# A graph layer on one core: five and four picked windows in turn for four, and 978 gathers for 1225

## The chip, the core and the metric

The kernel runs on one core of a Trainium2 chip. The metric is the device time of one execution in microseconds. The core has five engines: TensorE (PE; its weight loads are listed as PEld), VectorE (DVE), ScalarE (ACT), GpSimd (POOL) and SyncE (SP). Each works through its own list of instructions in order and waits for the others by semaphores.

## The reference

400,000 edges, sorted by `dst`, join 12,500 nodes with 128 features each. Every edge sends its source row through one of two linear maps, by its type; the messages are summed per destination; a self term is added, then relu, residual and a layer norm.

```python
Xs = X[src]
m_data = Xs @ W_data.T + b_data
m_ctrl = Xs @ W_control.T + b_control
msg = jnp.where((edge_types == 0)[:, None], m_data, m_ctrl)
agg = jax.ops.segment_sum(msg, dst, num_segments=X.shape[0])
out = agg + (X @ W_self.T + b_self)
x = _layernorm(x + jax.nn.relu(out), axis=-1)
```

## The kernel before, in words

The sum over edges is taken before the linear maps: for each node and type the kernel sums source rows, and multiplies by the weights once per node. `x` is split into three bf16 parts that add up to the float32 value and is held twice: in SBUF as `x3` (98 blocks of 128 nodes) and in DRAM as `rows3`.

**Tiles, groups, windows.** 128 edges make a tile; 3125 tiles make 25 groups `g` of 125 tiles, which cover 500 nodes each. A group is cut into windows, one after the other in `dst`: "p" windows of 12, 11, 11, 11 tiles (`PC`) and "e" windows of 20 tiles (`EC`), in turn. The two kinds get their source rows in two ways.

*Gathered* ("p", `gathered`): for each tile GpSimd issues an indirect DMA (L700) that fetches 128 rows from `rows3` into a `msg` tile, and PE adds them into a PSUM window `sums` by three matmuls with a one-hot matrix `psel` (L658) and one for the counts (L712). 1125 tiles go this way. The `msg` pool has `AHEAD` = 24 buffers; a gather is listed where its tile is used, and POOL may run ahead in its list as far as buffers are free.

*Picked* ("e", `picked`): PE itself takes rows out of `x3`. The 2560 edges of a window are sorted into 100 cells of 32 places, one cell per block of nodes (`give_slots`: a chain of DVE work with small PE products: `before` L537, `ranks` L547 on, `rank_matrix`, `over`, then `put` L601 and `spread` L609, which writes a table to DRAM and broadcasts it back as `pick`, 800 KB). Matmuls with the one-hot `pick` as weights give the rows in PSUM (`got` L732, 98 matmuls, four side by side), ACT casts them to bf16 (`emsg` L743, 12 casts of two row groups), and PE adds them into another `sums` window (L658, 72 matmuls and 3 for spares; counts L761). Up to 64 edges that find no place ("spares") are fetched by one gather on POOL (`last`, L747).

**Order.** One e window and the p tiles listed beside it are a *pair*; there are 100, and the work order is written out in Python: each stream yields units with a place between 0 and 1, and `merged` sorts them by place. `picked` has seven units (steps): unit t lists the `got` matmuls and casts of four row groups, the counts and the `sums` of the unit before; the seventh unit has no `got`, only the last `sums`, the `tiled` work of a later window at key 6 (`turn_codes` L621, the spares' `turn` L489 and `keep_codes` L631, L496, L498) and `accumulate`. Meanwhile the slots of the window two pairs ahead are computed. Tiles of p windows start at pair `LAG` = 2.

`got` has two PSUM buffers of two banks, `sums` two of one bank, `emsg` five buffers, `esel` and `psel` (one-hot matrices from DVE, L463) two each. `accumulate` (L688) adds a finished `sums` window into `acc[g]` on DVE at an offset read from `place_i`; `finish` multiplies by the weights, normalizes and writes 500 rows (L837, L850 and on).

**First part.** ACT's queue loads `x` and the weights, SP the indices: first `dst` of every window (`first_i`, from which DVE computes `halves` L340, `node0` and `place_i`), `near_i`, the edges of group 0. `x` is split while the slots of windows 0 and 1 are made; then `rows3` is stored.

Of the kernel before, what the change touches and what calls it, by code (L numbers as in the profile page):

```python
# [17 lines left out]
P = 128  # L18
D = 128
# [6 lines left out]
PC = (12, 11, 11, 11)  # L26
PB = 12
EC = 20
CQ = EC // 4
NE = len(PC)  # L30
# [6 lines left out]
AW = PW + DPC * (PB - 1)  # L37
# [9 lines left out]
AHEAD = 24  # L47
ACC_ROWS = 99 * P
EPS = 1e-5

assert sum(PC) + NE * EC == GC and NC % GC == 0 and NBLK == NCELL - 2 and max(PC) == PB

# [16 lines left out]
):  # L69

# [78 lines left out]
def short_path(ctx, tc, const, ident, eps, wT, brow, bad, x, src, dst, etype, ws, bs, out):  # L149
# [12 lines left out]
    def windows(g):  # L162

        c = g * GC
        for i, n in enumerate(PC):
            yield "p", i, c, n
            yield "e", i, c + n, EC
            c += n + EC
# [4 lines left out]
    rows_p = NE * PB  # L173
    raw = {}
    starts = {k: [c for kind, _, c, _ in windows(0) if kind == k] for k in "pe"}
    assert all(b - a == 31 for k in "pe" for a, b in zip(starts[k][k == "p":], starts[k][1 + (k == "p"):]))

    def load(g, kind):
        names = ("src", "dst", "typ")
        if kind == "e":  # L180
            raw[kind, g] = [ld.tile([P, NE, EC], I32, name=f"e{name}") for name in names]
            c = g * GC + starts["e"][0]
            for t, a in zip(raw[kind, g], (src, dst, etype)):
                at = a[c * P:(c + 31 * (NE - 1)) * P].rearrange("(i k) -> i k", k=31 * P)[:, :EC * P]
                nc.sync.dma_start(out=t[:, :NE - 1, :], in_=at.rearrange("i (p c) -> p i c", c=EC))
                nc.sync.dma_start(out=t[:, NE - 1, :], in_=edges(a, c + 31 * (NE - 1), EC))
        else:
            raw[kind, g] = [ld.tile([rows_p, P], I32, name=f"p{name}") for name in names]
            c = g * GC
            for t, a in zip(raw[kind, g], (src, dst, etype)):  # L190
                nc.sync.dma_start(out=t[:PB, :], in_=a[c * P:(c + PB) * P].rearrange("(c p) -> c p", p=P))
                for i in range(1, NE):
                    b = c + starts["p"][i]
                    nc.sync.dma_start(
                        out=t[i * PB:(i + 1) * PB, :], in_=a[b * P:(b + PB) * P].rearrange("(c p) -> c p", p=P)
                    )


    first_i = keep.tile([1, NG, NWIN], I32, name="first_i")

    def load_first(kind):
        for i, (k, _, c, _) in enumerate(windows(0)):
            if k == kind:
                nc.sync.dma_start(
                    out=first_i[:, :, i:i + 1],
# [9 lines left out]
    for kind, i, c, _ in windows(0):  # L215
        if kind == "p":
            nc.sync.dma_start(
                out=near_i[i * PB:(i + 1) * PB, :],
                in_=dst.rearrange("(o g e) -> o g e", o=1, g=NG)[:, :, c * P].to_broadcast([PB, NG]),
            )  # L220
# [52 lines left out]
    for i, (w, b) in enumerate(zip(ws, bs)):  # L273
        nc.scalar.dma_start(out=wn[:, i, :], in_=w)
        nc.scalar.dma_start(out=brow[:, i, :], in_=b.rearrange("(o d) -> o d", o=1))
# [59 lines left out]
    over_n = keep.tile([P, NG * NE], BF, name="over_n")  # L335

    halves = tmp.tile([1, 2, NG * NWIN], I32, name="halves")
    nc.vector.memset(x3[:, NBLK - 1], 0.0)
    first = first_i.rearrange("o g w -> o (g w)")
    nc.vector.tensor_single_scalar(halves[:, 0, :], first, 7, op=OP.logical_shift_right)  # L340
    nc.vector.tensor_single_scalar(halves[:, 1, :], first, 127, op=OP.bitwise_and)
    halves_b = tmp.tile([1, 2, NG * NWIN], BF, name="halves_b")
    nc.vector.tensor_copy(halves_b, halves)
    fin0 = ps1.tile([P, 512], FP, name="fin")
    for i in range(2):
        nc.tensor.matmul(fin0[:, :NG * NWIN], scale[:, i, :], halves_b[:, i, :], start=(i == 0), stop=(i == 1))
    node0 = keep.tile([P, NG, NWIN], FP, name="node0")
    nc.vector.tensor_copy(node0, fin0[:, :NG * NWIN].rearrange("p (g w) -> p g w", w=NWIN))
    near = keep.tile([rows_p, NG], FP, name="near")
    from_i = tmp.tile([rows_p, 1], I32, name="from_i")  # L350
    from_f = tmp.tile([rows_p, 1], FP, name="from_f")
    nc.gpsimd.iota(from_i, pattern=[[0, 1]], base=-PAD, channel_multiplier=DPC)
    nc.vector.tensor_copy(from_f, from_i)
    for k in range(1, NE):
        ge = raw[f"ge{k}"] = tmp.tile([rows_p, 1], FP, name=f"ge{k}")
        nc.vector.tensor_scalar(
            ge, from_f, float(DPC * PB * k - PAD), float(-DPC * PB), op0=OP.is_ge, op1=OP.mult
        )
    for k in range(1, NE):
        nc.vector.tensor_add(from_f, from_f, raw.pop(f"ge{k}"))  # L360
    nc.vector.tensor_scalar(near, near_i, from_f, None, op0=OP.add)
    place = tmp.tile([1, 2, NG, NWIN], FP, name="place")
    ref = tmp.tile([1, NG, NE, 2], I32, name="ref")
    nc.gpsimd.iota(ref, pattern=[[GN, NG], [0, NE], [-PAD, 2]], base=PAD - M0, channel_multiplier=0)
    ref = ref.rearrange("o g e k -> o g (e k)")
    least = tmp.tile([1, NG, NWIN], FP, name="least")
    for i, (_, _, c, _) in enumerate(windows(0)):
        nc.vector.memset(least[:, :, i:i + 1], float(max(0, c * DPC - PAD)))
    nc.vector.tensor_tensor(place[:, 0], first_i, ref, op=OP.subtract)
    nc.vector.tensor_tensor(place[:, 1], place[:, 0], least, op=OP.max)  # L370
    nc.vector.tensor_scalar(place[:, 1], place[:, 1], float(R - WMAX), None, op0=OP.min)
    place_i = keep.tile([1, NG, NWIN], I32, name="place_i")
    nc.vector.tensor_copy(place_i, place[:, 1])
    nc.vector.tensor_tensor(place[:, 0], place[:, 0], place[:, 1], op=OP.not_equal)
    nc.vector.tensor_reduce(worst[0:1, 2, 0:1], place[:, 0].rearrange("o g w -> o (g w)"), AX.X, OP.max)

    wps = ps1.tile([P, 512], FP, name="fin")
    for i in range(3):
        nc.tensor.transpose(wps[:, i * D:(i + 1) * D], wn[:, i, :], ident)
    nc.scalar.copy(wT, wps[:, :3 * D].rearrange("p (i d) -> p i d", d=D))  # L380
# [36 lines left out]
    def prep_p(g):  # L417
# [6 lines left out]
        def first():  # L424
            nc.vector.tensor_copy(sf, s)
            nc.vector.tensor_scalar(rel, d, near[:, g:g + 1], None, op0=OP.subtract)
# [12 lines left out]
    def prep_e(g):  # L439
# [3 lines left out]
        for i in range(NE):  # L443
            cs = slice(i * EC, (i + 1) * EC)
            nc.vector.tensor_scalar(rel[:, cs], d[:, cs], node0[:, g, 2 * i + 1:2 * i + 2], None, op0=OP.subtract)
# [59 lines left out]
    def give_slots(w):  # L505
        g, i = divmod(w, NE)
# [127 lines left out]
        s["tiled"] = {5: [put, spread], 6: [turn_codes, keep_codes]}  # L634
# [13 lines left out]
    acc, added = {}, []  # L648
# [27 lines left out]
    def pass_on(g):  # L676

        if g + 1 < NG:
# [3 lines left out]
    def accumulate(g, i, ps, wide, width):  # L682

        begin_acc(g)
        with tc.issue_after(added[-2].ins) if len(added) > 1 else ExitStack():
            at = nc.vector.value_load(place_i[0:1, g, i:i + 1], min_val=0, max_val=R - WMAX)
        win = acc[g][:, :, bass.ds(at, width)]
        added.append(nc.vector.tensor_add(win, win, ps[:, :4 * wide].rearrange("p (a w) -> p a w", w=wide)[:, :, :width]))  # L688

    def gathered(g, i):  # L690
        n = PC[i]
        s = {}

        def choose():
            sel = sp.tile([P, n, 2 * PW], BF, name="psel")
            s["sel"] = select(sel, near_col, codes["p", g][1][:, i * PB:i * PB + n])

        def chunk(c):
            msg = mp.tile([P, 3 * D], BF, name="msg")
            nc.gpsimd.indirect_dma_start(  # L700
                out=msg, out_offset=None, in_=rows3[:, :],
                in_offset=bass.IndirectOffsetOnAxis(ap=codes["p", g][0][:, i * PB + c:i * PB + c + 1], axis=0),
            )
# [7 lines left out]
            add_rows(rows, msg, sel, c == 0, c == n - 1)  # L711
# [6 lines left out]
    def picked(w, tiled):  # L718

        g, i = divmod(w, NE)  # L720
# [44 lines left out]

        def unit(t):

            if t < turns:
                for q in range(t * per, (t + 1) * per, pair):
                    rows(q)  # L770
            if t == 0:
                choose(0)
            if t == 1:
                choose(8)
# [3 lines left out]
            if 0 < t < turns:  # L778
                for q in range((t - 1) * per, t * per if t < turns - 1 else NQ):
                    count(q)  # L780
            if t < turns:
                for u in tiled.get(t, []):
                    u()
            if t == turns - 1:
                last_rows()
            if t > 0:
                for q in range((t - 1) * per, t * per if t < turns else NQ):
                    add_rows(cells_of(s["ps"], EW, 0), s["msg"].pop(q), s["sel"][q], False, q == NQ - 1)
            if t == turns:
                for u in tiled.get(t, []):  # L790
                    u()
                accumulate(g, 2 * i + 1, s["ps"], EW, EW)

        turns = (NQ - 1) // per
        return evenly([lambda t=t: unit(t) for t in range(turns + 1)])
# [3 lines left out]
    soon = {NE - 2: (0, 1), NE - 1: (2, 3, 4)}  # L799
    assert (starts["p"][NE - 1]) * DPC - PAD >= 2 * (P - 3)  # L800
# [86 lines left out]
    pairs = NG * NE  # L887
# [14 lines left out]

    prep_e(0)
    merged(evenly(all_slots(0) + all_slots(1)), evenly(split_units))
# [5 lines left out]
    mp = ctx.enter_context(tc.tile_pool(name="msg", bufs=AHEAD))  # L910
# [6 lines left out]
    for u in prep_p(0):  # L917
        u()


    chunks, closed, rest = {}, {}, []
    for p in range(pairs):
        g, i = divmod(p, NE)
        for c, (_, u) in enumerate(gathered(g, i)):
            at = LAG + (p + (c + 0.5) / PC[i]) * (pairs - LAG) / pairs
            chunks.setdefault(int(at), []).append((at % 1, u))
        closed.setdefault(int(at), []).append(p)

    for w in range(pairs):
        g, i = divmod(w, NE)  # L930
# [3 lines left out]
        if i == 2 and g + 1 < NG:  # L934
# [9 lines left out]
        if w + 3 < pairs:  # L944
            more += [(0.55, lambda: [u() for u in begin_slots(w + 3)])]
# [178 lines left out]
```

## Time and profile before

| | |
|---|---|
| runs before | 2387.49 us median of 3 (2369.49 to 2400.51) |
| the profiled execution | 2371.03 us, its span 2369.3 us, mean granted clock 0.909 |
| PE, DVE, ACT, POOL busy | 1863.1, 1584.0, 1229.7, 1412.5 us |
| first `got` of pair 0, 1, 2 | 76.7, 93.2, 142.6 us |
| first `got` of pair 98, 99 | 2323.9, 2338.2 us |
| gathers on POOL | 1125 of tiles (mean 1147 ns) and 100 of spares (mean 1181 ns) |

The profile is of one execution. Busy times are sums over the span; matmuls overlap and their ends are modelled, so PE's busy time is no measure of its full rate. Lines read: source line, engine, operation, output <- input, count, then busy us, mean ns, idle us before, and what ended most of that idle time. In the timeline an entry is start, length, engine, line, operation, count, and in brackets the idle time before it with what ended it. "issue" is time in which an engine waited for nothing that the profile shows.

### The profile page before, as it was taken

The page shows a single profiled execution, that of the slowest core. Times are in us where ns is not written, and L with a number is a line of the kernel's source. Part 1 is how long each engine was busy: PE and PEld are TensorE (multiplying, and loading weights), DVE is VectorE, ACT ScalarE, POOL GpSimd, SP SyncE. Part 2 cuts the span into 40 slices and gives each one's busy share as a digit, 9 for nine tenths or more (in the row PEclk, how much of TensorE's full clock was granted, in tenths as well). Part 3 has the DMA queues.
Part 4 walks back from the last instruction along what each step waited for, and adds up shares of the span by engine and source line. Part 5 has one row for each costly group of instructions (what it writes and reads, how often), then busy time and mean ns, then how long its engine had stood idle before and what let it go on. Part 6 is the DMA issues. An engine that isn't in the chain of part 4 may idle for free.

```text
span 2369.3 us, 70786 instructions
## 1 busy us (share of the span) xinstructions
PE 1863.1 (79%) x28867; PEld 1364.9 (58%) x28867; DVE 1584.0 (67%) x4224; ACT 1229.7 (52%) x2322; POOL 1412.5 (60%) x1243
## 2 busy tenths in 40 slices
PE   0468887887878787888888887888888888887977
PEld 0346665665556565666565565665666665665646
DVE  6747676766666666767676766676667666676753
ACT  3435554555445545545555554555555555545635
POOL 0366665756465565665666665566666665676661
PEclk9879898999889899999999988998989999999979
DMA  7423342333333333333323323333323323233321
GB/s 206 148 80 104 97 107 84 109 91 98 87 96 96 100 100 90 109 97 94 108 85 106 107 86 102 97 98 106 107 83 104 102 88 102 89 101 105 97 87 42
DMA packets 185017, 236.73 MB, mean 100 GB/s; under 512 B 80295, under 2 KB 152282, under 8 KB 184682
## 3 DMA queue, kind: packets, MB, share of 16 engines
q0 software_dynamic: 57200, 115.59, 17.7%
q1 hardware_dynamic: 114418, 109.94, 14.8%
q10 hardware_dynamic: 13064, 6.60, 1.0%
q8 instruction: 228, 3.74, 0.7%
q14 instruction: 107, 0.88, 0.1%
HBM read 215.35 MB, written 16.64 MB: 98 GB/s over the span
## 4 chain that ended last, share of the span: by engine, by line
PE 66%; issue 10%; ACT 10%; DVE 6%; another core or an unknown queue 5%; DMA 1%; SPq 1%; DVEq 0%; ACTq 0%; POOL 0%; POOLq 0%
PE sums L658 32%; PE got L732 22%; ACT emsg L743 9%; PE fin L850 3%; PE rk L601 2%; PE sums L761 2%; PE rk L489 1%; PE sums L712 1%; DVE esel L463 1%; PE rk L537 1%; DVE x L249 1%; PE rk L621 1%; DVE xt L247 0%; PE fin L837 0%
## 5 line engine op out<-in xcount | busy, mean ns | idle before, releaser
L700 POOL DMA_INDIRECT msg<-rows,pidx x1125 | 1290.4, 1147 | 790.3 <-PE sums L658 363.4
L743 ACT CAST emsg<-got 128x768 bf16<-128x768 f32 x1200 | 919.8, 804 | 796.5 <-PE got L732 328.8
L732 PE MATMUL got<-x,pick 128*32 128x384 bf16 x9800 | 659.2, 353 | 238.7 <-ACT emsg L743 145.6
L658 PE MATMUL sums<-esel,emsg 128*128 128x176 bf16 x7200 | 751.3, 255 | 48.6 <-issue 46.0
L658 PEld LDWEIGHTS <-emsg 128*128 128x128 bf16 x7200 | 579.8, 104 | 220.0 <-issue 215.4
L463 DVE TENSOR_TENSOR esel<-code_col,code 128x1408 bf16<-128x1408 bf16 (+1 forms) x300 | 275.0, 917 | 348.9 <-PE sums L658 195.7
L732 PEld LDWEIGHTS <-pick 128*32 128x32 bf16 x9800 | 242.3, 97 | 421.3 <-issue 336.0
L658 PE MATMUL sums<-psel,msg 128*128 128x48 bf16 x3375 | 240.0, 187 | 48.0 <-issue 35.3
L658 PEld LDWEIGHTS <-msg 128*128 128x128 bf16 x3375 | 187.8, 99 | 77.6 <-issue 72.5
L747 POOL DMA_INDIRECT last<-rows,idx x100 | 118.1, 1181 | 139.4 <-DMA pdst<-in_dst_dram 91.4
L712 PE MATMUL sums<-psel,one_col 128*128 128x48 bf16 x1125 | 184.5, 185 | 16.9 <-issue 16.8
L688 DVE TENSOR_TENSOR acc<-acc,sums 128x352 f32 (+1 forms) x200 | 94.0, 470 | 132.5 <-PE sums L658 54.0
L761 PE MATMUL sums<-esel,one_col 128*32 128x176 bf16 x2500 | 168.2, 254 | 16.2 <-issue 14.7
L463 DVE TENSOR_TENSOR O<-cell_col,blk 128x2000 bf16<-128x2000 bf16 x100 | 119.3, 1193 | 55.7 <-PE got L732 27.8
L643 DVE TENSOR_SCALAR pick<-pick,lane_f 128x1600 bf16<-128x1600 bf16 x200 | 125.6, 642 | 14.2 <-DMA pick<-there 13.7
L601 PE MATMUL rk<-rv,O 128*128 128x64 bf16 x2000 | 89.0, 198 | 50.3 <-DVE rv L589 35.0
L761 PEld LDWEIGHTS <-one_col 128*32 128x32 bf16 x2500 | 84.2, 103 | 63.7 <-issue 31.1
L547 DVE TENSOR_REDUCE ahead<-rk 128x100 bf16<-128x500 f32 x100 | 67.5, 675 | 78.7 <-PE got L732 55.7
L712 PEld LDWEIGHTS <-one_col 128*128 128x128 bf16 x1125 | 109.6, 97 | 18.0 <-issue 17.7
L551 DVE TENSOR_TENSOR prod<-O,ahead 128x2000 bf16<-128x2000 bf16 x100 | 119.0, 1190 | 0.0
L601 PEld LDWEIGHTS <-O 128*128 128x128 bf16 x2000 | 73.4, 101 | 67.3 <-issue 54.8
L631 ACT CAST code<-rk 128x50 bf16<-128x50 f32 x100 | 20.3, 203 | 173.8 <-PE got L732 68.0
(170 smaller groups left out, 1998.4 us busy)
## 6 DMA issues: line engine op xcount, KB each, us to landing
pick<-there SPq DMA_DIRECT2D x100, 800.0 KB
msg<-rows,pidx POOLq DMA_INDIRECT x1125
rows<-x SPq DMA_DIRECT2D x6, 1344.0 KB
xs<-in_x_dram SPq DMA_DIRECT2D x99, 62.5 KB
out_dram<-h SPq DMA_DIRECT2D x99, 62.5 KB
xt<-in_x_dram ACTq DMA_DIRECT2D x6, 896.0 KB
psrc<-in_src_dram SPq DMA_DIRECT2D x100, 6.0 KB
pdst<-in_dst_dram SPq DMA_DIRECT2D x100, 6.0 KB
```

The costliest lines, as they stand in the source:

```text
L463: nc.vector.tensor_tensor(sel.rearrange("p n (w t) -> p n w t", t=2), col[:rows].rearrange("p (o w t) -> p o w t", o=1, t=2).to_broadcast( ...
L551: nc.vector.tensor_tensor(prod, s["O"], ahead.rearrange("p (o j) -> p o j", o=1).to_broadcast([P, EC, NCELL]), op=OP.mult)
L601: nc.tensor.matmul(s["rk"][:m, :2 * CAP], s["held"][:, c * NCELL:c * NCELL + m], s["rv"][:, c].rearrange("p v r -> p (v r)"), start=(c == ...
L643: nc.vector.tensor_scalar(t, t, lane_f, None, op0=OP.is_equal)
L658: nc.tensor.matmul(out, msg[:, j * D:(j + 1) * D], sel, start=(start and j == 0), stop=stop, skip_group_check=True)
L688: added.append(nc.vector.tensor_add(win, win, ps[:, :4 * wide].rearrange("p (a w) -> p a w", w=wide)[:, :, :width]))
L700: nc.gpsimd.indirect_dma_start(out=msg, out_offset=None, in_=rows3[:, :], in_offset=bass.IndirectOffsetOnAxis(ap=codes["p", g][0][:, i * P ...
L712: nc.tensor.matmul(cnt, one_col, sel, start=False, stop=(c == n - 1), skip_group_check=True)
L732: nc.tensor.matmul(ps[CAP * a:CAP * (a + 1), :], slots[w]["pick"][:, a * NQ + q, :], x3[:, 4 * q + a - a0].rearrange("p j d -> p (j d)"), ...
L743: nc.scalar.copy(msg, ps[:, :, :3 * D])
L747: nc.gpsimd.indirect_dma_start(out=msg[:OVF, :], out_offset=None, in_=rows3[:, :], in_offset=bass.IndirectOffsetOnAxis(ap=slots[w]["idx"], ...
L761: nc.tensor.matmul(cells_of(s["ps"], EW, 1)[CAP * (q % 4):CAP * (q % 4 + 1), :], one_col[:, :CAP], s["sel"][q], start=(q < 4), stop=(q + 4 ...
```

## The change

Every p window now has 5 tiles (`PB`), and a group five e windows of 20; but in odd groups the fifth e window is joined to the p window before it, which then has 25 tiles (`PL`). So 13 groups have five picked windows and 12 have four: 113 pairs. 865 tiles are gathered, and with 113 spare gathers POOL issues 978. Gathers are listed 14 tiles before their use (`AHEAD`) into 18 buffers (`HOLD`). `picked` has six units, and its last sums, the `tiled` work of key 6 and `accumulate` go into `ending`, which the first unit of the next pair calls after its `got` matmuls; `put` moves from unit 5 to unit 4, `spare_rows` from unit 1 to unit 2, and `prep_p` of the next group from pair 2 to pair 1 of a group. In the first part the weights move from ACT's queue to SP's, the first `dst` of e and p windows get tiles of their own, `near`, `place_i` and the weights' transposes are made at the end of the split, and the first piece of `x` is split ahead of all else.

```diff
-PC = (12, 11, 11, 11)
-PB = 12
+PB = 5
+PL = 25
-NE = len(PC)
+NE = 5
-AHEAD = 24
+SB = 1
+HOLD = 18
+AHEAD = 14
...
+    def of_p(g, i):
+        return PL if g % 2 and i == NE - 1 else PB
+    each_e = [(g, i) for g in range(NG) for i in range(NE - g % 2)]
...
-    first_i = keep.tile([1, NG, NWIN], I32, name="first_i")
+    first_i = {k: keep.tile([1, NG, NE], I32, name=f"first_{k}") for k in "ep"}
...
-        nc.scalar.dma_start(out=wn[:, i, :], in_=w)
-        nc.scalar.dma_start(out=brow[:, i, :], in_=b.rearrange("(o d) -> o d", o=1))
+        nc.sync.dma_start(out=wn[:, i, :], in_=w)
+        nc.sync.dma_start(out=brow[:, i, :], in_=b.rearrange("(o d) -> o d", o=1))
...
-        s["tiled"] = {5: [put, spread], 6: [turn_codes, keep_codes]}
+        s["tiled"] = {4: [put, spread], 6: [turn_codes, keep_codes]}
...
+    to_fetch = [(g, i, c) for g in range(NG) for i in range(NE) for c in range(0, of_p(g, i), SB)]
+    fetched = []
+    def fetch():
+        if to_fetch:
+            g, i, c = to_fetch.pop(0)
+            msg = mp.tile([P, SB, 3 * D], BF, name="msg")
+            for k in range(min(SB, of_p(g, i) - c)):
+                at = i * PB + c + k
+                nc.gpsimd.indirect_dma_start(...)
+            fetched.append(msg)
...
         def chunk(c):
-            msg = mp.tile([P, 3 * D], BF, name="msg")
-            nc.gpsimd.indirect_dma_start(...)
+            if c % SB == 0:
+                fetch()
+                s["msg"] = fetched.pop(0)
...
         def unit(t):
-            if t < turns:
-                for q in range(t * per, (t + 1) * per, pair):
-                    rows(q)
...
+            for q in range(t * per, (t + 1) * per, pair):
+                rows(q)
+            if t in (0, 1):
+                choose(8 * t)
+            if t == 0:
+                ending()
+            if t == 2:
                 spare_rows()
...
+        def end():
+            add((turns - 1) * per, NQ)
+            for u in tiled.get(turns, []):
+                u()
+            accumulate(g, 2 * i + 1, s["ps"], EW, EW)
...
+    split_units.pop(0)()
     prep_e(0)
-    merged(evenly(all_slots(0) + all_slots(1)), evenly(split_units))
+    merged([(0.97, places_and_weights)], evenly(all_slots(0) + all_slots(1)), evenly(split_units))
...
+    for _ in range(AHEAD):
+        fetch()
...
+        units, ending = picked(w, tiled, ending)
```

## Prediction

> **What bounds the kernel now.** I read the page first: the busy shares, then the chain that ended last.
>
> ```profile
> span 2369.3 us, 70786 instructions
> PE 1863.1 (79%) x28867; PEld 1364.9 (58%) x28867; DVE 1584.0 (67%) x4224; ACT 1229.7 (52%) x2322; POOL 1412.5 (60%) x1243
> PE 66%; issue 10%; ACT 10%; DVE 6%; another core or an unknown queue 5%; DMA 1%; SPq 1%; DVEq 0%; ACTq 0%; POOL 0%; POOLq 0%
> L700 POOL DMA_INDIRECT msg<-rows,pidx x1125 | 1290.4, 1147 | 790.3 <-PE sums L658 363.4
> ```
>
> PE carries two thirds of the chain, POOL nothing: its gathers mostly wait for PE to free a buffer (363.4 us). Taken so, the change is wrong: it moves 260 tiles from the engine at 60% to the one at 79%. But 15% of the chain is time that no shown work explains ("issue", "unknown queue"), so I went on to the pace of single pairs. A pair starts at its first `got` matmul in the timeline. From pair 2 (142.6) to pair 98 (2323.9) that is 2181.3/96 = 22.72 us each. Some are far off, and the stages show what differs:
>
> ```profile
> core 0: us, PE busy (x) PEld busy (x) DVE busy (x) ACT busy (x) POOL busy (x), PEclk, DMA share, GB/s
> 142.60:157.80 15.20, 15.01 (x284) 11.61 (x280) 13.88 (x35) 10.46 (x20) 13.64 (x5) 1.00 0.20 65
> 157.80:188.00 30.20, 22.32 (x290) 14.00 (x290) 16.10 (x49) 11.46 (x22) 21.18 (x20) 0.77 0.33 93
> 2229.30:2246.20 16.90, 15.47 (x288) 11.73 (x284) 14.01 (x34) 11.79 (x27) 7.80 (x6) 1.00 0.34 98
> 2246.20:2278.70 32.50, 24.07 (x283) 14.99 (x280) 13.96 (x33) 10.30 (x21) 21.05 (x19) 0.68 0.34 97
> 2301.60:2323.90 22.30, 19.09 (x316) 15.24 (x314) 14.71 (x46) 12.40 (x27) 13.24 (x12) 1.00 0.30 92
> 2323.90:2338.20 14.30, 13.89 (x258) 10.59 (x259) 5.40 (x11) 10.23 (x19) 1.33 (x1) 1.00 0.29 88
> ```
>
> Each row is one pair (start, end and length, then the engines' busy time): the same matmuls, but 15 to 17 us where POOL got 5 or 6 gathers through and 30 to 33 us where it got 19 or 20; the granted clock falls from 1.00 to 0.7. Is POOL the cause, or does a long pair merely leave room for more gathers? The pair at 2229.3 tells, since there POOL was held by something outside PE, the indices of the next group (`pcol`):
>
> ```profile
> 2238.99 0.95 POOL L700 DMA_INDIRECT msg<-rows,pidx  x1 [6.66 <-ACT pcol L414]
> ...
> 2262.81 0.94 POOL L700 DMA_INDIRECT msg<-rows,pidx  x1 [0.30 <-issue]
> 2264.06 0.94 POOL L700 DMA_INDIRECT msg<-rows,pidx  x1 [0.30 <-issue]
> ```
>
> PE ran through undisturbed while POOL stood still. Then POOL caught up, a gather every 1.25 us, and PE fell to one or two matmuls at a time with nothing shown to wait for:
>
> ```profile
> 2262.24 0.75 PE L658 MATMUL sums<-esel,emsg 128*128 128x176 bf16 x4 [0.54 <-issue]
> 2263.65 0.45 PE L658 MATMUL sums<-esel,emsg 128*128 128x176 bf16 x2 [0.67 <-issue]
> 2265.07 0.20 PE L658 MATMUL sums<-psel,msg 128*128 128x48 bf16 x1 [0.89 <-issue]
> ```
>
> So a gather has a price on PE that its own row does not show. The reading stands on few pairs; the rivals take that up.
>
> **The price of one gather.** Between the last two stages of that episode: (32.5 - 16.9)/(19 - 6) = 1.20 us. Between the first two pairs of the table: (30.2 - 15.2)/(20 - 5) = 1.00. Between the mean of the two quiet pairs (16.05 us, 5.5 gathers) and the mean pair (22.72 us; 1225/100 = 12.25 gathers and some 0.6 that straddle a border): 6.67/7.35 = 0.91. The pair with one gather (14.3) against its neighbour with 12 gives 8.0/11 = 0.73, but it has also lost the work on later pairs (DVE 5.4 instead of 14.7). The changed pair lies between the quiet and the mean one, so I take 0.9. The upper end is 1.2; the lower is 0, if gathers only follow the pace. Below nothing is excluded: one gather less adds no work to any engine.
>
> The Trainium skill speaks against it: "SBUF — State Buffer", section "SBUF: two separate sides", says that on the engines' side only the port pair that VectorE and GpSimd share contends, and that PE and ACT never wait on another engine there. By that rule the price is 0 and the sum 2510 us, by the rows 0.9 and 2155. The rows above disagree with the rule, or have a cause that it doesn't speak of.
>
> **The change, part by part.**
> *Pairs and gathers.* 113 pairs for 100. Each brings 98 `got`, 75 `sums`, 25 counts and 36 smaller matmuls, 11.1 us of ACT, 14.6 us of DVE (their rows for the pick path, 1107.5 and 1462.8 us, over 100), 2 DMA issues on SP with one 800 KB broadcast, and one spare gather. The mean pair holds all that, so pairs x pace counts it. Gathers per pair: 1225/100 = 12.25 before, 978/113 = 8.65 after: 3.6 x 0.9 = -3.24 us.
> *PE's own work on gathered tiles.* 11.25 per pair before, 865/113 = 7.65 after. Two neighbours in the timeline start 0.10 us apart:
>
> ```profile
> 1204.86 0.24 PE L658 MATMUL sums<-psel,msg 128*128 128x48 bf16 x3
> ...
> 1204.96 0.23 PE L658 MATMUL sums<-psel,msg 128*128 128x48 bf16 x3
> ```
>
> 3.6 x 0.10 = -0.36.
> *Finishing.* 25 batches as before over more pairs: the rows of L837 and L850 are 162 us, 1.62 a pair and then 1.44: -0.19.
> *Joined steps.* At the end of a pair PE adds the last rows while ACT has no cast to do, and ACT then stands before `code`:
>
> ```profile
> 1220.17 0.83 PE L732 MATMUL got<-x,pick 128*32 128x384 bf16 x16
> ...
> 1221.40 0.20 ACT L631 CAST code<-rk 128x50 bf16<-128x50 f32 x1 [2.97 <-PE sums L658]
> ```
>
> In the quiet pair of 142.6 the seventh step took 3.27 us and the next first step 1.46, 4.73 together. Joined, PE has 16 `got` (0.66), 27 `sums` at 0.073 (2.0) and the two short turns (0.5): 3.2, a gain of 1.5. Over all pairs the two take 3.67 + 2.37 = 6.0, so up to 2 may go. The lower end is 0, where the chain through DVE takes over. I take 0.9: ACT's casts (0.80 each, two a step) still set a floor of 1.6 in every step.
> *Gathers listed in front.* Eighteen buffers for 24, listed 14 tiles ahead: 14 x 18/7.65 = 33 us before use, far more than POOL's hold of 6.66 above. PE waited 2.1 us in all for gathers before; I price it at nothing, and a hold of POOL over 33 us would return in full. The spare gather stands one step later, `put` one step earlier; both have a step (some 3 us) of room.
> *38 more adds into acc* (238 for 200) of about 0.42 us and index work on 100 columns for 80 lie on DVE, which has 14 to 15 us of work in a pair of 18; without that room 38 x 0.42/113 = 0.14 a pair. The 3 more loads a group on SP (0.4 each) lie in SP's waits for `cell` (997.8 us).
> Pair: 22.72 - 3.24 - 0.36 - 0.19 - 0.9 = 18.03 us.
> *New first part.* DVE's first real work waited for first indices which stood behind other loads on SP:
>
> ```profile
> 18.06 0.25 DVE L340 TENSOR_SCALAR halves<-first_i 1x200 int32<-1x200 int32 x1 [4.53 <-DMA first_i<-in_dst_dram]
> ```
>
> Now only the five "e" ones, first on SP, are waited for; the other places and the weights (six issues, 2.5 us of ACT's queue, now on SP behind 15 index loads) are not needed until the end of the part. That is worth up to 8 us, or nothing where the loads of `x` set the end. Pairs 0 and 1 ended at 142.6 in a burst of 26 gathers (96 to 132 us); now 14 are listed, then two spare ones that pair 0's end waits for: (16 x 1.25) = 20 us after the stored rows, so about (96 - 8) + 20 = 108, and 20 more for pair 1. I put pair 2 at 130 (120 to 143).
> Sum: 130 + 109 pairs (2 to 110) x 18.03 = 1965, + the tail as before, 2369.3 - 2323.9 = 45.4: 2140. Around the span lie 1.7 us (2371.03): 2142. The profiled run is 0.7% under the median of the runs, 2387.49; times 1.007 this is 2157, rounded 2155.
>
> **Rivals.**
> 1. *Slower: gathers only follow PE.* Price 0: 21.27 x 109 + 177 = 2495, 2510 with the factor. For it: POOL is at 0% of the chain, and a longer pair has room for more gathers. Against it: the hold by `pcol`, which PE did not cause. It decides below a price of p where 109 x (21.27 - 3.6p) + 177 = 2371, p = 0.32. Chance 0.16.
> 2. *DVE takes PE's place.* It works 14 us a pair in order, and `esel` already idles 3.5 us a pair, mostly for PE's sums; its buffers now come free in the next pair's first step. If the join brings nothing and each pair gains 1 us there: 19.93 x 109 + 177 = 2349, 2366 with the factor: no change. Against it: DVE had 13.88 of 15.20 us in the quiet pair. Chance 0.14, a half of it under 2340.
> 3. *More than forecast.* Price 1.2 and a join of 1.5: 16.35 x 109 + 177 = 1959, 1973; with only one of the two about 2040. Chance 0.08.
>
> **How the numbers follow.** The forecast (2155; own range 2050 to 2300) has 0.62. The range of 2040 to 2400 leaves out rival 1 and the best of rival 3. Faster by over 2% (under 2340; 2% is about what runs of this kernel can tell): 0.62 + 0.08 + 0.06 = 0.76; within 2%: 0.08; slower: 0.16.
>
> **What would show it.** 113 pairs of about 18 us; POOL with 978 gathers and some 1130 us busy; pair 2 near 130; no 2.97 us hole of ACT between pairs; a mean clock over 0.909; fewer "issue" and "unknown" shares. If pairs stay at 21 us with 8 or 9 gathers each, the price was wrong; at 19 to 20 us with `esel` waiting longer, the join was.

## The result, and the profile after

The changed kernel takes 2159.6 us (median of four runs, 2150.6 to 2164.9) where the kernel before takes 2378.5 in the same comparison: a ratio of 0.908, 95% interval 0.902 to 0.913. The forecast was 2155. That ratio belongs to the chip on which it was measured: on another chip of the same type it is 0.995 (e9). The experiments are mostly about this difference.

The page of the profile after, the lines that answer to those of before:

```profile
span 2163.1 us, 75401 instructions
PE 1860.4 (86%) x30869; PEld 1392.9 (64%) x30869; DVE 1730.8 (80%) x4707; ACT 1359.2 (63%) x2556; POOL 1305.9 (60%) x996
PE 61%; DVE 19%; ACT 9%; issue 5%; DMA 2%; another core or an unknown queue 1%; POOL 1%; DVEq 0%; SPq 0%; ACTq 0%; POOLq 0%
L715 POOL DMA_INDIRECT msg<-rows,pidx x865 | 1155.4, 1336 | 752.8 <-PE sums L671 316.3
```

PE has 2002 more matmuls and is busy for 2.7 us less. What went is time without shown work: "issue" and "unknown queue" fall from 15% of the chain to 6%. VectorE comes up from 6% to 19%: it is next in line. A gather's own row got longer, 1336 ns for 1147, so POOL is busy for 1305.9 us, not for the 1130 that were said. It grows on the quicker chips told of below too, from 1192 (e12) to 1314 ns (e9). The Trainium skill ("SBUF — State Buffer", section "SBUF: two separate sides") has GpSimd's descriptor writes wait while VectorE, in a two-port mode, holds the port pair that they share. VectorE's busy share did rise, but no run here tells that this is the cause.

Three pairs of the changed kernel in the stage view (length, then busy time of PE, weight loads, DVE, ACT, POOL, the granted clock, DMA share, GB/s); they got 25, 7 and 11 gathers:

```profile
103.17:142.35 39.18, 18.19 (x260) 13.67 (x260) 16.06 (x47) 10.10 (x17) 25.96 (x25) 0.70 0.34 92
744.58:760.84 16.26, 14.82 (x267) 11.20 (x264) 12.53 (x31) 10.12 (x19) 12.64 (x7) 1.00 0.34 93
1894.07:1915.75 21.68, 17.55 (x265) 12.61 (x262) 12.81 (x31) 10.10 (x19) 13.08 (x11) 0.84 0.27 90
```

A pair with many gathers is still long at a low clock, as before, but such pairs are rare now: from pair 3 to pair 110 none has more than 11 gathers started in it, where before 83 of 95 pairs had 12 or more. The seam between two pairs, from the timeline:

```profile
1207.01 0.83 PE L762 MATMUL got<-x,pick 128*32 128x384 bf16 x16
1208.24 0.18 ACT L644 CAST code<-rk 128x50 bf16<-128x50 f32 x1
```

`code` has no idle time before it here (2.97 us in the example of before), and the next pair's rows are already out. Over all pairs the time from ACT's last cast of a pair to the first of the next falls from 4.7 to 1.5 us.

### The profile page after: what moved, and what is told of

The parts are those of the page before. It is cut to its first block, busy times and chain, and to the rows that moved or that the text cites. A ratio compares the mean times of both kernels' runs of the same rounds, so it can differ in the third digit from the quotient of the medians.

```text
span 2163.1 us, 75401 instructions
## 1 busy us (share of the span) xinstructions
PE 1860.4 (86%) x30869; PEld 1392.9 (64%) x30869; DVE 1730.8 (80%) x4707; ACT 1359.2 (63%) x2556; POOL 1305.9 (60%) x996
## 4 chain that ended last, share of the span: by engine, by line
PE 61%; DVE 19%; ACT 9%; issue 5%; DMA 2%; another core or an unknown queue 1%; POOL 1%; DVEq 0%; SPq 0%; ACTq 0%; POOLq 0%
PE sums L671 27%; PE got L762 22%; ACT emsg L773 6%; PE rk L614 3%; DVE esel L476 3%; PE fin L885 2%; PE sums L791 2%; DVE prod L564 2%; DVE rv L602 1%; DVE pick L656 1%; PE rk L502 1%; PE rk L550 1%; DMA pick<-there 1%; DVE found L573 1%
## 5 line engine op out<-in xcount | busy, mean ns | idle before, releaser
L715 POOL DMA_INDIRECT msg<-rows,pidx x865 | 1155.4, 1336 | 752.8 <-PE sums L671 316.3
L773 ACT CAST emsg<-got 128x768 bf16<-128x768 f32 x1356 | 1035.8, 802 | 513.3 <-PE got L762 310.0
L762 PE MATMUL got<-x,pick 128*32 128x384 bf16 x11074 | 713.3, 335 | 136.8 <-ACT emsg L773 110.6
L671 PE MATMUL sums<-esel,emsg 128*128 128x176 bf16 x8136 | 782.6, 244 | 6.1 <-issue 5.8
L476 DVE TENSOR_TENSOR esel<-code_col,code 128x1408 bf16<-128x1408 bf16 x339 | 308.8, 911 | 43.9 <-PE sums L671 36.2
L703 DVE TENSOR_TENSOR acc<-acc,sums 128x352 f32 (+2 forms) x238 | 102.0, 428 | 211.6 <-PE sums L671 153.3
L671 PE MATMUL sums<-psel,msg 128*128 128x48 bf16 x2595 | 188.0, 185 | 9.5 <-issue 5.0
L777 POOL DMA_INDIRECT last<-rows,idx x113 | 146.2, 1294 | 70.6 <-DVE idx L513 24.4
L671 PEld LDWEIGHTS <-msg 128*128 128x128 bf16 x2595 | 150.9, 98 | 21.0 <-issue 16.1
L476 DVE TENSOR_TENSOR O<-cell_col,blk 128x2000 bf16<-128x2000 bf16 x113 | 135.0, 1194 | 21.6 <-PE got L762 10.7
L741 PE MATMUL sums<-psel,one_col 128*128 128x48 bf16 x865 | 145.9, 184 | 3.8 <-issue 3.7
L791 PEld LDWEIGHTS <-one_col 128*32 128x32 bf16 x2825 | 99.2, 98 | 51.5 <-issue 18.2
```

The lines of the kernel that those rows point to most:

```text
L476: nc.vector.tensor_tensor(sel.rearrange("p n (w t) -> p n w t", t=2), col[:rows].rearrange("p (o w t) -> p o w t", o=1, t=2).to_broadcast( ...
L671: nc.tensor.matmul(out, msg[:, j * D:(j + 1) * D], sel, start=(start and j == 0), stop=stop, skip_group_check=True)
L715: nc.gpsimd.indirect_dma_start(out=msg[:, k, :], out_offset=None, in_=rows3[:, :], in_offset=bass.IndirectOffsetOnAxis(ap=codes["p", g][0] ...
L741: nc.tensor.matmul(cnt, one_col, sel, start=False, stop=(c == n - 1), skip_group_check=True)
L762: nc.tensor.matmul(ps[CAP * a:CAP * (a + 1), :], slots[w]["pick"][:, a * NQ + q, :], x3[:, 4 * q + a - a0].rearrange("p j d -> p (j d)"), ...
L773: nc.scalar.copy(msg, ps[:, :, :3 * D])
```

## The experiments

The runs fell on four chips, and beside each group of them the kernel before ran on the same chip. The chips are of two kinds. The kernel before takes 2434.6 us on chip 0 and 2383.0 on chip 14, as in the profile shown first: kind A. It takes 1986.7 and 1985.0 us (at two times) on chip 1 and 1967.8 on chip 5: kind B. The expectations of e1 to e8 were written before this was known, with the times of kind A in mind.

**e1 to e4, on chip 1 (before: 1986.7).** e1 is the changed kernel with four picked windows in every group:

```diff
-        return PL if g % 2 and i == NE - 1 else PB
+        return PL if i == NE - 1 else PB
-    each_e = [(g, i) for g in range(NG) for i in range(NE - g % 2)]
+    each_e = [(g, i) for g in range(NG) for i in range(NE - 1)]
```

(From the order of its code, it finishes some nodes of the last group before their last windows are added; the work is otherwise as it should be.)

> The changed kernel, but with four picked windows in every group (100 pairs and 1125 + 100 gathers, as many as in the kernel before), so that only the joined steps, the new first part and the longer list stay. Theory (a gather costs PE 0.9 us, a gathered tile 0.10): the changed kernel's pace of 18.2 us with 8.65 gathers becomes 18.2 + 3.6 x 1.0 = 21.8 us with 12.25; 98 x 21.8 + 142 + 50 = 2330 us, 2290 to 2370. Rival (gathers only follow PE, the joined steps brought everything): pace stays at 18.2 to 18.6, 98 x 18.4 + 192 = about 2000 us.

Measured: 2052.0 us, ratio 1.033 (1.026 to 1.040): slower than the kernel before on this chip, and far under the theory's 2330. PE waits 186.5 us for `last`, the spare gather; in e2, with fewer gathers, 15.4 us.

e2 has five picked windows in every group: `of_p` returns `PB` always, and `each_e` runs over all `NE`.

> The changed kernel, but with five picked windows in every group: 125 pairs and 625 + 125 = 750 gathers. Theory: 6 gathers a pair instead of 8.65 take 2.65 x 1.0 off 18.2, so 15.6 us a pair, 123 x 15.6 + 192 = 2110 us, were it not for VectorE, which has 14.6 us of work in a pair; by the changed kernel's own pairs (17.2 us with 7 gathers, 18.3 with 9) a pair with 6 takes 16.7, 2245 us. So 2110 to 2250. Rival (price 0): 123 x 18.2 + 192 = 2430 us. Rival (VectorE sets the end from here on): above 2250.

Measured: 2109.9 us, ratio 1.061 (1.057 to 1.065). The number is at the lower edge of the range said, but not for the reason said: the kernel before is quicker here too. VectorE holds 52% of e2's chain and a pair takes 16.1 us, so VectorE sets the pace, as the last rival had it, though not above 2250.

e3 takes the joined steps out of the changed kernel:

```diff
-        return evenly([lambda t=t: unit(t) for t in range(turns)]), end
+        return evenly([lambda t=t: unit(t) for t in range(turns)] + [end]), lambda: None
```

> The changed kernel with the joined steps undone: the last rows and the accumulation stand in a seventh step of their own again. Theory: the join is worth 0.9 us a pair, 113 x 0.9 = 100 us, so 2260 us (2240 to 2290). If the join only moved work from one wait to another: 2160. If it was worth the 2 us that the steps allow at most: 2385.

Measured: 1964.5 us, ratio 0.987 (0.984 to 0.991).

e4 puts the joined steps into the kernel before: `ending` of the last pair is called in a pair's first step, after `choose(0)`, and the seventh step is gone.

> The kernel before with the joined steps alone (same 100 pairs and 1225 gathers, same first part, list as before). Theory: 0.9 us x 100 pairs off 2380, so 2290 us (2200 to 2330; the kernel e1 with four picked windows everywhere should be near it). If the join is worth nothing without fewer gathers: 2380. If gathers cost nothing and the join did all: about 2000.

Measured: 2070.7 us, ratio 1.041 (1.038 to 1.045): slower. PE waits 199.6 us for `last`, the spare gather, which the joined first step needs while POOL still has others ahead of it; that is 39 us more than in the kernel before on a chip of kind B (e12), of 84 us to explain. The rest is open.

Three of the four (e1, e3, e4) lie far below what the price of 0.9 us gives, the fourth fits for another reason, and in none of the four profiles does "issue" stand among PE's larger waits. That raised the question of what the gathers do on the first chip.

**e5 to e8, on chip 0 (before: 2434.6).** e5 and e6 are the kernel before with one gather for two tiles, or for a whole window:

```diff
-            msg = mp.tile([P, 3 * D], BF, name="msg")
-            nc.gpsimd.indirect_dma_start(
+            if c % 2 == 0:    # e6: c % 12
+                s["msg"] = mp.tile([P, 3 * D], BF, name="msg")
+                nc.gpsimd.indirect_dma_start(
...
+            msg = s["msg"]
```

> The kernel before with one gather for every two gathered tiles (600 + 100 gathers instead of 1125 + 100); PE, DVE and ACT do the same work, and every second tile uses the rows of the one before it, which is what it leaves out. Theory (0.9 us a gather): 525 x 0.9 = 470 us less, about 1900 us; a floor of 15 to 16 us a pair (the quiet pairs) would give 1700 to 1800. Rival (gathers only follow PE): 2370, unchanged.

> The kernel before with one gather for a whole window of 11 or 12 tiles (100 + 100 gathers); the other tiles use its rows, which is what it leaves out. PE, DVE and ACT do the same work. Theory: 1025 x 0.9 = 920 us less by the price alone, but DVE's 14.6 us and the quiet pairs' 15 us are a floor, so 1600 to 1750 us. Rival (price 0): 2370.

Measured: 2127.2 us, ratio 0.875 (0.860 to 0.891), and 1836.8 us, ratio 0.756 (0.742 to 0.770). PE, DVE and ACT do the same work as before; only gathers are gone. So a gather costs, and does not merely follow: 307/525 = 0.58 us each in e5, 598/1025 = 0.58 in e6. Both forecasts by 0.9 (about 1900, and 1600 to 1750) were too low. But the mean hides the form of the price. Three pairs in a row of e5, in the stage view, with 1, 17 and 7 gathers:

```profile
1894.89:1913.88 18.99, 18.57 (x322) 15.33 (x320) 16.73 (x50) 13.83 (x29) 1.17 (x1) 1.00 0.15 53
1913.88:1946.28 32.40, 22.48 (x284) 14.18 (x282) 13.71 (x33) 11.80 (x26) 17.74 (x17) 0.74 0.32 88
1946.28:1961.76 15.48, 15.19 (x281) 11.38 (x278) 13.65 (x33) 10.08 (x21) 11.04 (x7) 1.00 0.28 88
```

Seven gathers in a pair cost next to nothing (the first of the three is long because it also finishes nodes, 322 matmuls); seventeen cost (32.40 - 15.48)/(17 - 7) = 1.7 us for each one more. All of e5 from pair 3 on says the same: its 39 pairs with 4 to 7 gathers take 16.4 us on the mean, its 21 pairs with 12 or more take 29.1 us (28 pairs with up to 3 take 19.0; the finishing of nodes falls mostly into these). The price is that of gathers that follow one another closely. Four lines of that pair's timeline:

```profile
1924.15 0.95 POOL L701 DMA_INDIRECT msg<-rows,pidx  x1 [0.30 <-issue]
1924.87 0.27 PE L763 MATMUL sums<-esel,one_col 128*32 128x176 bf16 x3 [1.09 <-issue]
1925.41 0.94 POOL L701 DMA_INDIRECT msg<-rows,pidx  x1 [0.30 <-issue]
1926.31 1.05 PE L658 MATMUL sums<-esel,emsg 128*128 128x176 bf16 x5 [0.99 <-issue]
```

e7 and e8 ask which part of a gather it is. They replace the 865 gathers of the changed kernel, by a plain load and by a memset:

```diff
-                nc.gpsimd.indirect_dma_start(
-                    out=msg[:, k, :], out_offset=None, in_=rows3[:, :],
-                    in_offset=bass.IndirectOffsetOnAxis(ap=codes["p", g][0][:, at:at + 1], axis=0),
-                )
+                nc.sync.dma_start(out=msg[:, k, :], in_=rows3[at * P:at * P + P, :])    # e7
+                nc.gpsimd.memset(msg[:, k, :], 0.0)                                     # e8
```

(In e7 `at` is first shifted by `(g * 45) % 90`, so that the blocks loaded differ from group to group.)

> The changed kernel with its 865 gathers of edge rows replaced by plain loads of the same 128 rows x 768 bytes, issued by SP, into the same buffers (it leaves out the choice of the rows). The transfers' bytes stay, GpSimd's work on the indices goes (113 spare gathers are left). If the price comes with the transfer into SBUF: 2160 us, unchanged. If it comes with GpSimd's making of the gather: 113 x 15 + 190 = about 1900 us (1850 to 1980).

> The changed kernel with its 865 gathers of edge rows replaced by a GpSimd memset of the same buffers (it leaves out the rows themselves): GpSimd still writes SBUF between the same waits, no transfer is made. If the price comes with the gather in either of its parts (indices or transfer): 1850 to 1980 us, as few as with plain loads or fewer. If it comes with any work of GpSimd beside PE and its waits: 2160.

Measured: 1962.6 us, ratio 0.807 (0.793 to 0.822), and 1958.5 us, ratio 0.806 (0.791 to 0.820). The changed kernel as it is was not run on chip 0; by its ratio of 0.908 it would take about 2210 there. The DMA queues of the changed kernel (first two lines; packets, MB, share of 16 engines) and of e7 (last two) show that the 85 MB only changed queue:

```profile
q1 hardware_dynamic: 125770, 121.51, 17.9%
q0 software_dynamic: 45136, 90.65, 15.1%
q1 hardware_dynamic: 250330, 206.60, 36.1%
q0 software_dynamic: 3616, 5.56, 1.3%
```

With the same bytes moved by plain loads the price is gone, and without any transfer the time is much the same; in both runs no "issue" row is left among PE's waits. So the price is neither the bytes moved nor GpSimd's plain writing into SBUF (865 memsets of 0.43 us each): it comes with GpSimd's making of an indirect transfer, or with what that transfer's queue does that a plain one does not. Those two were not separated. The form of the transfer goes with the queue: a plain load reads neighbouring rows, in 144 packets a tile where a gather has 48. The Trainium skill's page "Perfetto Trace Analysis" (section "DMA Instruction — SWDGE (GPSIMD)") says that a row of such a gather ends when the descriptors are made, not when the data has landed; by that the bursts that spoil PE's pace are seen at their source. No run here shows where such a row ends.

**e9 and e10, on chip 1 (before: 1985.0).** e9 is the changed kernel as it is, e10 is e3's kernel.

> The changed kernel again, beside the kernel before. Theory after e1 to e8: on the chip where the kernel before takes 2370 to 2435 us a gather holds PE's signals back, and the ratio is again 0.90 to 0.92; on the chip where it takes 1987 us it doesn't, VectorE sets the pace, and the changed kernel takes 1960 to 2000 us there, a ratio of 0.985 to 1.005. Rival (the price of a gather is the same everywhere, that call was quick for another reason): a ratio of 0.90 to 0.92 on either chip, 1800 us beside 1987.

> The changed kernel with the joined steps undone, beside the changed kernel itself. By the pace: of the 4.49 us that a pair lost, 3.6 gathers at the 0.585 us that e5 gave make 2.1, PE's own work and the finish 0.55; the 1.8 left would be the join, so 113 x 1.8 = 200 us over the changed kernel on the chip where a gather has a price (2360 beside 2160). By the forecast's 0.9: 2260. Rival (the join is worth nothing, the price of a gather is 1.1): 2160. On the chip without a price: 1965, the changed kernel within 2% of it.

Measured: e9 1972.6 us, ratio 0.995 (0.993 to 0.998); e10 1965.2 us, ratio 0.990 (0.988 to 0.993). Both are as forecast for a chip without a price. On a chip of kind B the change gains half a per cent, and its joined steps cost about as much; both lie within the 2% that the prediction counts as no change.

**e11, on chip 14 (before: 2383.0).** The same kernel without the joined steps.

> The changed kernel with the joined steps undone, once more, for the chip where the kernel before takes 2370 to 2435 us, to size the join there. If the join is worth the 1.8 us a pair that the other terms leave, 2360 us, a ratio of 0.99 to the kernel before; by the forecast's 0.9 us 2260, 0.95; if it is worth nothing 2160, 0.91. On the chip where that kernel takes 1985 us: 1965 again.

Measured: 2252.1 us, ratio 0.945 (0.938 to 0.952). The changed kernel was not run on this chip; at 0.908 it would take 2163, so the join is worth 89 us or 0.79 a pair: near the forecast's 0.9, not the 1.8 that I had come to after e5 by taking its mean price for every gather.

**e12, on chip 5 (before: 1967.8).** The kernel before, unchanged, for its profile on a chip of kind B.

> The kernel before, unchanged, for its profile on the chip where it takes 1985 us. Theory: there PE has next to no idle time of the kind 'issue' (188 us in the kernel before's first profile, over 2300 us), the matmuls after a burst of gathers run in groups of 16 and not in ones and twos, and a pair takes 2 us less than GpSimd lets it only where GpSimd's 12.25 gathers x 1.25 us = 15.3 us bind; pace about 18.6 us. Rival (that chip is just quicker at everything): single matmuls, casts and gathers are shorter by a sixth too. On the other chip: 2380 again.

Measured: 1972.6 us, ratio 1.003 (0.999 to 1.007), 18.69 us a pair from pair 3 on (22.8 in the first profile). Its page:

```profile
span 1964.6 us, 70786 instructions
PE 38%; DVE 30%; DMA 19%; issue 5%; POOL 3%; ACT 2%; SPq 1%; DVEq 1%; ACTq 0%; POOLq 0%
L743 ACT CAST emsg<-got 128x768 bf16<-128x768 f32 x1200 | 904.2, 803 | 284.5 <-PE got L732 273.5
```

The cast takes 803 ns here and 804 in the first profile, a `got` matmul 348 and 353, a `sums` matmul of picked rows 243 and 255, a gather's median 0.96 and 0.95 us. So that chip is not quicker at each thing, as the rival had it. ACT's idle time before its casts falls from 796.5 to 284.5 us. And the waits of PE (who waits, for whom, us in all, times, the longest), the three largest of the kernel before in its first profile, and then the three largest of e12 and its row for the casts:

```profile
PE got L732 <- ACT emsg L743: 145.6, 192, 8.4
PE sums L658 <- issue: 87.1, 186, 4.6
PE got L732 <- issue: 80.9, 134, 2.8
```

```profile
PE sums L658 <- DMA last<-rows,idx: 160.8, 51, 13.7
PE rk L601 <- DVE rv L589: 47.8, 15, 19.8
PE fin L346 <- DVE from_f L353: 20.4, 1, 20.4
PE got L732 <- ACT emsg L743: 7.0, 23, 0.8
```

In e12 PE has no "issue" row at all. (The expectation put them at 188 us on kind A; the five largest make 214: 87.1, 80.9, 16.8, 14.8 and 14.7.) The same spacing of gathers leaves PE alone, in e12's timeline:

```profile
430.05 0.94 POOL L700 DMA_INDIRECT msg<-rows,pidx  x1 [0.30 <-issue]
431.30 1.02 POOL L700 DMA_INDIRECT msg<-rows,pidx  x1 [0.30 <-issue]
431.46 0.83 PE L732 MATMUL got<-x,pick 128*32 128x384 bf16 x16
432.31 1.08 PE L658 MATMUL sums<-esel,emsg 128*128 128x176 bf16 x12
```

A gather every 1.25 us, and PE goes on in groups of 16 and 12. In e5, on kind A, such a stretch has ones, threes and fives.

What kind B has instead is a wait for gathers to come. PE waits 160.8 us for spare gathers that stand behind others, and only 14.6 us in e9. From pair 3 on a pair's time grows by 1.08 us with each gather that starts in it (correlation 0.89), which is near the 1.25 us in which POOL gets one out. That GpSimd itself limits these pairs is read from this and not shown: a long pair also has room for more gathers, and no run took gathers alone away on this kind. The change takes most of that wait away and meets VectorE. The chain of e9:

```profile
DVE 53%; PE 29%; ACT 6%; issue 4%; DMA 4%; DVEq 1%; POOL 1%; SPq 1%; ACTq 0%; POOLq 0%
```

A pair takes 16.55 us in e9. 113 x 16.55 = 1870, 100 x 18.69 = 1869: the 13 pairs more eat what each pair gains. And e7 and e8, on kind A without those gathers, run at 16.46 us a pair from pair 3 on, the pace of kind B with them (16.55, e9). So with its gathers the changed kernel is 1.7 us a pair slower on kind A (18.23) than on kind B, and without them it keeps kind B's pace to 0.1 us. Kind B without them was not run.

## Why the prediction was right, and where it was not

The mechanism held on the kind of chip that it was read from: there gathers cost PE time, and the joined steps save some. Step by step, on kind A, with profiles of two chips (the changed kernel's first one, and e11's of chip 14):

- *The price of a gather, 0.9 us.* Without the join a pair takes 19.14 us (e11, from pair 3 on) against 22.8 before: 3.66. Less the 0.36 and 0.19 of PE's own work, which were not measured alone, that is 3.11/3.6 = 0.86. This is a remainder: it holds all that the change did to a pair beside the join, the listing of the gathers in front too. By the mean price of e5 and e6 (0.58) the 3.6 gathers make 2.1 us, and no run separates the other 1.0; e1, which keeps all the gathers, ran on kind B. That 0.9 came out because the changed pair lies between the quiet and the mean one, from which it was taken, fits, but is not shown. As a price of any gather it is wrong: in e5 it is near 0 for spread gathers and 1.7 us in a burst.
- *The join, 0.9 us.* 19.14 - 18.23 = 0.91 by the paces of the two profiled executions, 0.79 by the medians of the times. The ceiling of 2 was out of reach: the first step grew from 2.4 to 2.9 us on the mean, and 1.35 us pass between the last `got` of a pair and the first of the next. Together that is 4.3 us where the kernel before has 6.0, but in e11, without the join, it is 4.9 already.
- *The pace.* 18.23 us from pair 3 on, 18.03 forecast: 108 x 0.2 = 21.6 us more.
- *The first part.* Pair 2 was forecast at 130 and began at 103.2. That step failed in its form: the burst did not hold pair 0's and pair 1's end, it moved into pair 2, which took 39.18 us with 25 gathers. Pair 3 began at 142.3 where the forecast has 130 + 18 = 148, so that the size was off by 5.7 us.
- *The tail.* 2163.1 - 2111.4 (pair 111) = 51.7 us, 45.4 forecast: 6.3 more. It is 49.7 to 51.5 us in e3, e9, e10 and e11 too, so neither the kind of chip nor the join makes it; what does is open.
- *The sum.* 2140 - 5.7 + 21.6 + 6.3 = 2162, the span is 2163.1. The factor of 1.007 for the profiled execution did not return (2164.9 against a median of 2159.6); the 15 us that it added stood in by chance for most of the 22 us missing in the sum.

The rivals. The first (price 0) is false on kind A by e5 to e8. On kind B PE has no such idle time, and yet the rival's time does not follow: it kept the pace and added 13 pairs, while there each pair lost 2.1 us (18.69 to 16.55), where PE's wait for spare gathers alone had been 1.6 (160.8 us over 100 pairs). The second (DVE takes over) is wrong on kind A, where `esel` lost most of its idle time (44 us in all for 349), and right on kind B, where DVE is 53% of the chain.

The rule that I weighed against the price ("SBUF — State Buffer", section "SBUF: two separate sides" of the Trainium skill: PE and ACT never wait on another engine on the engines' side of SBUF) is not contradicted by this: with a memset by POOL in the gathers' place the kernel takes 1958.5 us (e8), with no such work of POOL 1962.6 (e7). What makes PE late is something that the rule doesn't speak of.

What I could not see from one chip: all that speaks for the price in the first profile belongs to that chip. The forecast is right there in its sum, with the gathers' step known only as a remainder, and would have been wrong by 9% on chip 1 (1972.6 us). That the comparison fell on a chip of kind A again was luck: of the four chips tried later two are of the other kind.

## What to carry to other kernels

Where a profile shows "issue" gaps on an engine beside another engine's bursts, find a stretch where that other engine stands still, and then thin its work out or replace it by work of another kind: that told cause from consequence here, and nothing in the page did. Price such a burden by the pairs that resemble the changed one, since here it grew with crowding more than with the count (e5). And before trading one engine's work for another's, time the kernel before on a second chip: a trade that wins 9% on one may be worth nothing on the next, and the best version may differ (without the join 0.990 against 0.995 on chip 1, but 0.945 on chip 14 against 0.908 in the first comparison).

## What was not expected of the hardware

- Two kinds of chip: the same program takes 2383 to 2435 us on chips 0 and 14 and 1968 to 1987 on chips 1 and 5, with the cast, a `got` matmul and a gather's median equal within 2%. Whether this is a property of the chips or of what they were doing at the time is open; chip 1 gave 1987 and 1985 us in two separate calls.
- On kind A, indirect gathers 1.25 us apart make PE's matmuls come in ones and threes with 0.4 to 1.1 us of "issue" before them. In such pairs the granted clock is 0.68 to 0.77; in two pairs of kind B with 19 and 17 gathers it is 0.83 and 0.87, without "issue" rows. What lowers it was not tried. Plain loads of as many bytes break up PE's matmuls in no such way (ratio 0.807), nor does a memset by GpSimd (0.806).
- Which of GpSimd's making of an indirect transfer and that transfer's queue holds PE back, and by what path, was not tried.
